# Masked weights transposed in quarters, the last pair amid the first unit of products

## Chip, cores, metric

One core of one Trainium2 chip. The time is that of the device in microseconds (us); of several runs the median is given.

## The reference

`x` is (128, 32, 128): 128 batches of 32 tokens with 128 features; `cond_8` is (128, 8). Two layers, each added to its input, in 32-bit floats:

```python
# layer 0: a weight matrix for each batch, mixed from 8 masked ones
masked_w = weight * mask[None, :, :]                  # (8, 128, 128)
w_bot = jnp.einsum('bg,got->bot', y, masked_w)        # y = cond_8
x = x + (jnp.einsum('bnt,bot->bno', x, w_bot) + bias)
# layer 1: 8 experts, the top 2 of softmax(cond_8) for each batch, and a shared MLP
rw = softmax(cond_8); w, sel = top_k(rw, 2); w = w / w.sum(-1)
out = sum over e of dense_w[:, e] * gemma_mlp(x, skill_gate[e], skill_up[e], skill_down[e])
x = x + out + gemma_mlp(x, shared_gate, shared_up, shared_down)
```

`gemma_mlp` is `(gelu(x @ gate) * (x @ up)) @ down` with 512 hidden features.

## The kernel before, in words

All data lie transposed, with features on the 128 partitions and the 4096 tokens along the free side. The work has a short opening (layer 0 for all batches, with the routing of the experts done beside it on VectorE) and a long rest (the shared MLP over eight tiles of 512 tokens, and tiles of gathered tokens for the experts), which is TensorE work almost without a pause. The order of instructions on each engine is the order of the program text: the schedule is written out by hand, and generators (`make_weights`, `routing`) let parts of one step be put between parts of another.

The change touches the opening only. Its steps:

- **Loads** (L89 to L96). SP issues the conditions, the mask and three eighths of the weights `w0_sb`; ScalarE's queue issues the other five eighths.
- **Warm-up** (`warm_up`, L105). Products of ones with ones into a bank that nobody reads, six at L109 and three at L217. Each appears as two records on TensorE.
- **`spread_cond`** (L220). VectorE spreads the transposed conditions in `ps_y` into `yd`, which is what the products of the units stream: the first 32 batches at L230, the other 96 at the end of `transpose_weights` (L262).
- **Masks** (L238 to L245). VectorE multiplies the weights by the mask into `mw`, in two halves of 512 elements per partition.
- **Transposes** (`transpose_weights`, L248). Eight transposes of 128x128 on TensorE, in pairs; each pair goes to one PSUM bank, and the bank is copied to `wT` (L261), pair 0 and 2 by ScalarE, 1 and 3 by VectorE. The four banks come from the pools `ps_g` and `ps_u` in turn.
- **Units** (`make_weights`, L271). A unit makes half of the weights of 32 batches. It takes four banks, and for each of four values of `k` issues four matrix products, one for each group of 32 rows (`j`), each into another bank; a 32-bit product is two records, so that a unit has 32. Products of different row groups run beside each other. Then the four banks are evicted to `W` with a reordering copy: `j` = 0 and 2 by ScalarE (L294), `j` = 1 and 3 by VectorE (L292). Unit 1 reads the first half of `wT` (pairs 0 and 1), unit 2 the second (pairs 2 and 3), and so on in turn for the next 32 batches.
- **Banks.** PSUM has eight: two in the pool `ps_g`, three in `ps_u`, three in `ps_o`. In a pool the buffers are handed out in turn. `bank` (L266) takes the next pool from `ring` (L264), the names "guouoguo" repeated. A tile can be written once the buffer's former tile has been read for the last time. `warm` took a buffer of `ps_u` and `ps_y` one of `ps_o`.
- **`apply_weights`** (L297). For a tile of 512 tokens, 16 batches, products of `W` with the tokens (L303), copied by ScalarE to `z`; `finish_cond` (L316) transposes `z` back and adds bias and tokens. Three units come first, then the tiles 0 and 1 (which need units 1 and 2), some routing steps (`advance`), then the second `hold_loads` (L182, a memset by VectorE which SP waits for), the loads of the shared weights, two more units, and so on (L760 to L778).

Of the kernel before, what the change touches and what calls it, by code (L numbers as in the profile page):

```python
# [10 lines left out]
F32 = mybir.dt.float32  # L11
# [19 lines left out]
def kernel(  # L31
# [16 lines left out]
    nc = tc.nc  # L48
    P = 128
    D, NT = xT.shape  # L50
    B, G = cond.shape
# [21 lines left out]
    const = ctx.enter_context(tc.tile_pool(name="const", bufs=1))  # L73
# [8 lines left out]
    ps_g = ctx.enter_context(tc.tile_pool(name="ps_g", bufs=2, space=PSUM))  # L82
    ps_u = ctx.enter_context(tc.tile_pool(name="ps_u", bufs=3, space=PSUM))
# [16 lines left out]
    ident = const.tile([P, P], F32, name="ident")  # L100
# [4 lines left out]
    def warm_up(n):  # L105
        for _ in range(n):
            nc.tensor.matmul(warm[:, 0:P], ones, ones, start=True, stop=True)
# [50 lines left out]
    OQ = RG // G  # L158
    NJ = P // RG
    OB = OQ * NJ  # L160
    NQ = P // OB
# [52 lines left out]
    nc.tensor.transpose(  # L214
        ps_y[:, 0:B], cond_rep.rearrange("b j g o -> b (j g o)"), ident
    )
    warm_up(3)  # L217
    yd = const.tile([P, B, OQ], F32, name="yd")

    def spread_cond(b0, n):  # L220
        nc.vector.tensor_tensor(
            yd[:, b0 : b0 + n, :],
            ps_y[:, b0 : b0 + n].unsqueeze(2).to_broadcast([P, n, OQ]),
            own4.unsqueeze(1).to_broadcast([P, n, OQ]),
            ALU.mult,
        )

    QB = TB // P
    NB = TB // (QB * OQ)
    spread_cond(0, NB)  # L230


    NR = P // OQ
    mw = const.tile([P, NR, G, OQ], F32, name="mw")
    w0_r = w0_sb.rearrange("p g (r o) -> p r g o", o=OQ)
    mask_r = mask_sb.rearrange("p (r o) -> p r o", o=OQ)
    NRH = NR // 2
    for half in range(2):  # L238
        rows = ts(half, NRH)
        nc.vector.tensor_tensor(  # L240
            mw[:, rows, :, :],
            w0_r[:, rows, :, :],
            mask_r[:, rows, :].unsqueeze(2).to_broadcast([P, NRH, G, OQ]),
            ALU.mult,
        )  # L245
    wT = const.tile([P, NQ, P], F32, name="wT")

    def transpose_weights():  # L248
        TQ = QB // 2
        for i in range(NQ // TQ):  # L250
            pool, tag = (ps_u, "u") if i % 2 else (ps_g, "g")
            pt = pool.tile([P, TQ * P], F32, name="pt", tag=tag)
            for k in range(TQ):
                q = i * TQ + k
                nc.tensor.transpose(  # L255
                    pt[:, ts(k, P)],
                    mw[:, ts(q, NJ), :, :].rearrange("p j g o -> p (j g o)"),
                    ident,
                )
            copy = nc.vector.tensor_copy if i % 2 else nc.scalar.copy  # L260
            copy(wT[:, ts(i, TQ), :].rearrange("p q t -> p (q t)"), pt)  # L261
        spread_cond(NB, B - NB)  # L262

    ring = itertools.cycle("guouoguo")  # L264

    def bank(name):  # L266

        pool, tag = {"g": (ps_g, "g"), "u": (ps_u, "u"), "o": (ps_o, "acc")}[next(ring)]
        return pool.tile([P, TB], F32, name=name, tag=tag)

    def make_weights(i, half):  # L271

        banks = [bank(f"w_{j}") for j in range(NJ)]
        q0 = half * QB
        for k in range(QB):
            for j in range(NJ):
                rows = slice(j * RG, (j + 1) * RG)
                nc.tensor.matmul(  # L278
                    banks[j][:, ts(k, NB * OQ)],
                    wT[rows, q0 + k, :],  # L280
                    yd[rows, ts(i, NB), :].rearrange("p b o -> p (b o)"),
                    start=True,
                    stop=True,
                )
        yield
        for j in range(NJ):
            dst = W[:, ts(i, NB), q0 * OB : (q0 + QB) * OB].rearrange(
                "p b (k o) -> p k b o", k=QB
            )[:, :, :, ts(j, OQ)]
            src = banks[j].rearrange("p (k b o) -> p k b o", k=QB, o=OQ)  # L290
            if j % 2:
                nc.vector.tensor_copy(dst, src)  # L292
            else:
                nc.scalar.copy(dst, src)  # L294
        yield
# [312 lines left out]
    class Pipeline:  # L608
# [31 lines left out]
        def copy(self):  # L640
            other = Pipeline(self.h_pool)
            other.pending = list(self.pending)
            return other
# [15 lines left out]
    def shared_tile(t, widths=None):  # L659
        def finish(ps, part):  # L660
            w = part.stop - part.start
            cols = slice(t * TB + part.start, t * TB + part.stop)
            if t < EARLY:
                nc.vector.tensor_tensor(acc[:, cols], ps[:, 0:w], x1[:, cols], ALU.add)
            elif t < NTILE - 2:
                nc.vector.tensor_tensor(acc[:, cols], ps[:, 0:w], acc[:, cols], ALU.add)
            else:
                o = o_pool.tile([P, w], F32, name="o", tag="o")
                nc.vector.tensor_tensor(o, ps[:, 0:w], acc[:, cols], ALU.add)  # L669
                queue = nc.scalar if part.start else nc.sync  # L670
                queue.dma_start(out=outT[:, cols], in_=o)

        return Mlp(TB, x1[:, ts(t, TB)], shared, finish, widths)
# [76 lines left out]
        return mlp  # L750


    units = [make_weights(i, half) for i in range(B // NB) for half in range(2)]

    def weights():
        unit = units.pop(0)
        next(unit)
        next(unit)

    transpose_weights()  # L760
    PAIR = NB // BT
    for _ in range(3):
        weights()
    for i in range(2):
        for t in range(PAIR):
# [50 lines left out]
    between = shared_tile(EARLY)  # L816
# [90 lines left out]
```

## Time and profile before

| | |
|---|---|
| median of three runs | 285.27 us (285.13 to 285.67) |
| profiled execution | 284.8 us |
| its span, first to last instruction | 283.1 us |
| mean granted TensorE clock | 1.000 |
| TensorE busy | 277.5 us |
| first mask multiplication (L240) starts | 4.82 us |
| first product of a unit (L278) starts | 6.75 us |
| first eviction on VectorE (L292) starts | 7.99 us |
| first product of `apply_weights` (L303) starts | 10.57 us |

In the rows of the profile PE is TensorE's products, PEld its weight loads, DVE VectorE, ACT ScalarE, POOL GpSimd, SP the engine that issues most of the DMAs. A row of the timeline gives start and duration in us, engine, line, operation, the tiles written and read, their shape, the number of instructions merged in the row, and in brackets how long the engine was idle before and what it waited for. Instructions on TensorE overlap: a row's duration is from the start of its first to the end of its last, gaps between starts can hide in it. The chain of waits is followed back from the last instruction, at each step to what released it.

### The profile page before, as it was taken

To read this page: it belongs to the slowest core of one execution; us is meant where nothing else is said; L and a number is where in the kernel's file an instruction comes from. 1 tells how busy PE (TensorE), PEld (TensorE's weight loads), DVE (VectorE), ACT (ScalarE), POOL (GpSimd) and SP (SyncE) were. 2 spreads that over 40 slices of the span, in tenths; PEclk is the share of its full clock that TensorE was granted. 3 is DMA by queue.
4 is the path that set the end of the run, shared out by engine and by line. 5 is a ranking of instruction groups with operands and counts; after the bars stand their busy time and mean duration, and the time that the engine had idled before them with its cause. 6 is when DMAs were issued, how large, how long until landed. Compare 5 with 4: busy or idle time off the path is not lost.

```text
span 283.1 us, 5164 instructions
## 1 busy us (share of the span) xinstructions
PE 277.5 (98%) x1424; PEld 171.8 (61%) x1424; DVE 166.9 (59%) x489; ACT 78.8 (28%) x149; POOL 47.9 (17%) x285
## 2 busy tenths in 40 slices
PE   7999999999999999999999999999999999999994
PEld 6987545657657567576585665765557444444442
DVE  4897794546666666666566676666666733233232
ACT  5665123222222222222222222222222221222120
POOL 3001213423024220241222212421000000000000
PEclk9999999999999999999999999999999999999999
DMA  4381067334335435325253343432000020100101
GB/s 129 108 220 45 2 190 255 115 111 121 105 112 166 132 111 151 113 94 168 85 182 106 112 151 111 127 115 96 5 0 1 14 97 0 39 0 3 71 37 45
DMA packets 25763, 27.21 MB, mean 96 GB/s; under 512 B 1920, under 2 KB 16768, under 8 KB 25728
## 3 DMA queue, kind: packets, MB, share of 16 engines
q1 hardware_dynamic: 25440, 26.42, 29.9%
q10 hardware_dynamic: 288, 0.39, 0.5%
q8 instruction: 13, 0.21, 0.3%
q14 instruction: 22, 0.18, 0.2%
HBM read 24.71 MB, written 2.10 MB: 95 GB/s over the span
## 4 chain that ended last, share of the span: by engine, by line
PE 96%; DMA 1%; DVE 0%; SPq 0%; issue 0%; DVEq 0%
PE pg L580 30%; PE pu L580 30%; PE ps_out L598 29%; PE w L278 3%; PE pz L303 3%; PE pt L320 1%; DMA w_sb<-in_w0T_dram 1%; PE pt L255 0%; DVE mw L240 0%; PE ps_w L544 0%; SPq L92 0%; SPq L90 0%; DVE o L669 0%; PE ps_i L543 0%; PE ps_n L370 0%
## 5 line engine op out<-in xcount | busy, mean ns | idle before, releaser
L587 DVE TENSOR_TENSOR h<-ge,pu 128x384 f32<-128x384 f32 (+1 forms) x117 | 69.3, 592 | 76.4 <-PE pu L580 76.4
L585 ACT ACTIVATE ge<-pg 128x384 f32<-128x384 f32 (+1 forms) x117 | 61.4, 525 | 186.1 <-PE pg L580 175.7
L731 DVE SCALAR_TENSOR_TENSOR acc<-ps_out,slot_w,acc 128x32 f32 x260 | 65.1, 250 | 27.6 <-DVE h L587 17.1
L598 PE MATMUL ps_out<-h,wd 128*128 128x384 f32 (+2 forms) x216 | 70.3, 424 | 0.0
L580 PE MATMUL pu<-xg,wu 128*128 128x384 f32 (+2 forms) x216 | 70.0, 423 | 0.0
L580 PE MATMUL pg<-xg,wg 128*128 128x384 f32 (+2 forms) x216 | 70.0, 423 | 0.0
L710 POOL COPY xg<-x 128x32 f32 x260 | 41.9, 209 | 120.3 <-PE pu L580 96.3
L580 PEld LDWEIGHTS pg<-xg,wg 128*128 128x128 f32 x216 | 37.7, 190 | 19.8 <-issue 0.7
L598 PEld LDWEIGHTS ps_out<-h,wd 128*128 128x128 f32 x216 | 37.5, 190 | 20.1 <-DVE h L587 1.3
L580 PEld LDWEIGHTS pu<-xg,wu 128*128 128x128 f32 x216 | 37.6, 190 | 19.1
L580 PE MATMUL pg<-x,swg 128*128 128x512 f32 x64 | 32.8, 594 | 0.0
L580 PE MATMUL pu<-x,swu 128*128 128x512 f32 x64 | 32.7, 592 | 0.0
L598 PE MATMUL ps_out<-h,swd 128*128 128x512 f32 (+2 forms) x72 | 32.4, 545 | 0.0
L598 PEld LDWEIGHTS ps_out<-h,swd 128*128 128x128 f32 x72 | 13.3, 190 | 14.9 <-issue 12.4
L580 PEld LDWEIGHTS pu<-x,swu 128*128 128x128 f32 x64 | 12.2, 190 | 15.3 <-issue 15.1
L580 PEld LDWEIGHTS pg<-x,swg 128*128 128x128 f32 x64 | 11.8, 190 | 12.6 <-issue 11.7
L292 DVE COPY W<-w 128x512 f32<-128x512 f32 x16 | 9.9, 682 | 0.7 <-PE w L278 0.7
L294 ACT COPY W<-w 128x512 f32<-128x512 f32 x16 | 8.3, 598 | 3.7 <-PE w L278 3.7
L278 PE MATMUL w<-yd,wT 32*128 32x128 f32 x256 | 9.0, 279 | 0.0
L278 PEld LDWEIGHTS w<-yd,wT 32*128 32x128 f32 x256 | 8.2, 186 | 1.2 <-DVE x L321 0.8
L325 POOL COPY acc<-x 128x512 f32<-128x512 f32 x6 | 3.7, 614 | 29.7 <-DVE x L321 29.5
L303 PE MATMUL pz<-W,xin 128*32 128x128 f32 x256 | 7.8, 274 | 0.1
(99 smaller groups left out, 67.7 us busy)
## 6 DMA issues: line engine op xcount, KB each, us to landing
wg<-in_gate_dram SPq DMA_DIRECT2D x27, 256.0 KB, 2.8
wu<-in_up_dram SPq DMA_DIRECT2D x27, 256.0 KB, 2.9
wd<-in_down_dram SPq DMA_DIRECT2D x27, 256.0 KB, 2.8
xin<-in_xT_dram SPq DMA_DIRECT2D x6, 256.0 KB, 4.3
out_dram<-acc SPq DMA_DIRECT2D x4, 256.0 KB, 2.1
xin<-in_xT_dram SPq DMA_DIRECT2D x1, 512.0 KB, 6.5
out_dram<-acc SPq DMA_DIRECT2D x1, 512.0 KB, 2.6
w_sb<-in_w0T_dram ACTq DMA_DIRECT2D x1, 320.0 KB, 2.9
```

The source lines that it names most:

```text
L278: nc.tensor.matmul(banks[j][:, ts(k, NB * OQ)], wT[rows, q0 + k, :], yd[rows, ts(i, NB), :].rearrange("p b o -> p (b o)"), start=True, sto ...
L292: nc.vector.tensor_copy(dst, src)
L294: nc.scalar.copy(dst, src)
L303: nc.tensor.matmul(pz[j * N : (j + 1) * N, ts(k, P)], x_sb[t][:, ts(b, N)], W[:, t * BT + b, :], start=True, stop=True,)
L320: nc.tensor.transpose(pt[:, ts(k, P)], z[:, ts(k, P)], ident)
L325: nc.gpsimd.tensor_copy(acc[:, ts(t, TB)], x1[:, ts(t, TB)])
L580: nc.tensor.matmul(ps[:, ts(i, self.n)], w[:, ts(c, P)], self.x_in, start=True, stop=True,)
L585: nc.scalar.activation(ge[:, 0:n], pg[:, 0:n], AF.Gelu_apprx_tanh)
L587: nc.vector.tensor_tensor(h[:, 0:n], ge[:, 0:n], pu[:, 0:n], ALU.mult)
L598: nc.tensor.matmul(ps[:, 0 : cols.stop - cols.start], self.wd[:, c, :], h[:, i * self.n + cols.start : i * self.n + cols.stop], start=(c = ...
L710: nc.gpsimd.tensor_copy(xg[:, ts(j, N)], x1[:, bass.ds(v, N)])
L731: nc.vector.scalar_tensor_tensor(a, ps[:, ts(j, N)], slot_w[:, slot0 + j : slot0 + j + 1], a, ALU.mult, ALU.add,)
```

## The change

The masks are multiplied in four quarters instead of two halves. After each of the first three quarters its pair of transposes is issued. The fourth quarter's pair is issued in the middle of unit 1, between its second and third value of `k`. All four pairs are copied to `wT` by ScalarE: three ahead of unit 1, the fourth between the products and the evictions of unit 1. The second `spread_cond` follows the fourth mask. The four banks of the pairs are taken up front. The ring starts with "ouogguou" for units 1 and 2 and then goes on as before. The second warm-up has one product instead of three.

```diff
-    warm_up(3)
+    warm_up(1)
...
-    NRH = NR // 2
-    for half in range(2):
-        rows = ts(half, NRH)
+    wT = const.tile([P, NQ, P], F32, name="wT")
+    TQ = 2
+    TR = TQ * NJ
+    pts = [
+        pool.tile([P, TQ * P], F32, name="pt", tag=tag)
+        for pool, tag in ((ps_g, "g"), (ps_u, "u")) * (NQ // TQ // 2)
+    ]
+
+    def mask_weights(i):
+        rows = ts(i, TR)
         nc.vector.tensor_tensor(
             mw[:, rows, :, :],
             w0_r[:, rows, :, :],
-            mask_r[:, rows, :].unsqueeze(2).to_broadcast([P, NRH, G, OQ]),
+            mask_r[:, rows, :].unsqueeze(2).to_broadcast([P, TR, G, OQ]),
             ALU.mult,
         )
-    wT = const.tile([P, NQ, P], F32, name="wT")
-
-    def transpose_weights():
-        TQ = QB // 2
-        for i in range(NQ // TQ):
-            pool, tag = (ps_u, "u") if i % 2 else (ps_g, "g")
-            pt = pool.tile([P, TQ * P], F32, name="pt", tag=tag)
-            for k in range(TQ):
-                q = i * TQ + k
-                nc.tensor.transpose(
-                    pt[:, ts(k, P)],
-                    mw[:, ts(q, NJ), :, :].rearrange("p j g o -> p (j g o)"),
-                    ident,
-                )
-            copy = nc.vector.tensor_copy if i % 2 else nc.scalar.copy
-            copy(wT[:, ts(i, TQ), :].rearrange("p q t -> p (q t)"), pt)
-        spread_cond(NB, B - NB)
-
-    ring = itertools.cycle("guouoguo")
+
+    def transpose_weights(i):
+        for k in range(TQ):
+            nc.tensor.transpose(
+                pts[i][:, ts(k, P)],
+                mw[:, ts(i * TQ + k, NJ), :, :].rearrange("p j g o -> p (j g o)"),
+                ident,
+            )
+
+    def copy_transpose(i, copy):
+        copy(wT[:, ts(i, TQ), :].rearrange("p q t -> p (q t)"), pts[i])
+
+
+    ring = itertools.chain("ouogguou", itertools.cycle("guouoguo"))
...
-    def make_weights(i, half):
+    def make_weights(i, half, between=None):
...
         for k in range(QB):
+            if between and k == QB // 2:
+                between()
             for j in range(NJ):
...
-    units = [make_weights(i, half) for i in range(B // NB) for half in range(2)]
+    units = [
+        make_weights(i, half, None if (i, half) != (0, 0) else lambda: transpose_weights(3))
+        for i in range(B // NB)
+        for half in range(2)
+    ]
...
-    transpose_weights()
+    for i in range(3):
+        mask_weights(i)
+        transpose_weights(i)
+    mask_weights(3)
+    spread_cond(NB, B - NB)
+    for i in range(3):
+        copy_transpose(i, nc.scalar.copy)
+
+    unit = units.pop(0)
+    next(unit)
+    copy_transpose(3, nc.scalar.copy)
+    next(unit)
     PAIR = NB // BT
-    for _ in range(3):
+    for _ in range(2):
         weights()
```

## The prediction

> **What bounds the kernel now.** I read the page's busy table and its chain first, then the chain of waits up to 20 us in order of time, then the timeline of the first 12 us, the last one opened in windows of a few tenths of a us so that single instructions have their own start.
>
> ```profile
> PE 277.5 (98%) x1424; PEld 171.8 (61%) x1424; DVE 166.9 (59%) x489; ACT 78.8 (28%) x149; POOL 47.9 (17%) x285
> ...
> PE 96%; DMA 1%; DVE 0%; SPq 0%; issue 0%; DVEq 0%
> ```
>
> TensorE is busy 98% of the span and carries 96% of the chain. Nothing behind 10.57 us interrupts the chain for long, so whatever the change does to the time at which the products of `apply_weights` (L303) begin reaches the end of the kernel nearly undiminished. The opening decides. Its chain:
>
> ```profile
> 1.74 2.96 DMA w_sb<-in_w0T_dram
> ...
> 4.82 0.70 DVE mw L240
> ...
> 5.57 1.26 PE pt L255 x8
> 6.82 3.66 PE w L278 x94
> ...
> 10.57 1.95 PE pz L303 x64
> ```
>
> The weights land at 4.70, VectorE masks, TensorE transposes, the units of L278 follow. The row of 3.66 us hides what matters: a unit is 32 products, and the first takes from 6.753 to 7.748, so three would take 2.98 us plus tails. The timeline shows who is really late:
>
> ```profile
> 4.82 1.29 DVE L240 TENSOR_TENSOR mw<-w_sb,mask_sb 128x512 f32<-128x512 f32 x2 [0.21 <-DMA w_sb<-in_w0T_dram]
> ...
> 6.75 3.73 PE L278 MATMUL w<-yd,wT 32*128 32x128 f32 x96
> ...
> 7.94 2.05 ACT L294 COPY W<-w 128x512 f32<-128x512 f32 x4 [0.93 <-PE w L278]
> 7.99 3.68 DVE L292 COPY W<-w 128x512 f32<-128x512 f32 x6 [0.24 <-PE w L278]
> ...
> 10.57 1.95 PE L303 MATMUL pz<-W,xin 128*32 128x128 f32 x64
> ```
>
> VectorE's six evictions stand without a gap: start 7.986, ends 8.677, 9.273, 9.872, 10.468. The first waits for the end of the first unit. Call its start D = 7.986. `apply_weights(0)` needs the fourth eviction: 10.468, and its first weight load stands at 10.539, its first product at D + 2.58. Unit 3 needs banks that unit 1 held: its weight loads wait until 8.58 (ScalarE's eviction ended 8.530), 8.729 (VectorE's first, 8.677), 9.067 (ScalarE's second, 9.016) and 9.325 (VectorE's second, 9.273). From 9.325 it needs 0.885 us to its last product at 10.210. So TensorE could go on at about 10.41; the fourth eviction is later by 0.15. Two paths, 0.15 apart, both hung on D.
>
> **Masks in quarters.** Two multiplications of 512 elements (0.687 us, starts 0.609 apart) become four of 256. No row shows that one. The nearest is VectorE's copy of 128x256 at 0.424 us, with the next instruction 0.342 behind its start; half of 0.687 is the lower bound, 0.344. I take 0.42 and a spacing of 0.342: starts 4.82, 5.16, 5.50, 5.85, ends 5.24, 5.58, 5.93, 6.27. TensorE starts 0.052 behind a mask (5.511 to 5.563), and the second transpose of a group 0.165 behind its first: pairs at 5.29/5.46, 5.64/5.80, 5.98/6.14. The first half was done at 5.511 before.
>
> **Copies by ScalarE.** Four copies of 128x256 at 0.372 us replace two there and two on VectorE. ScalarE is free from 5.677. The first starts 0.037 behind its transpose's end (5.46 + 0.273), so 5.77 to 6.14, the next 6.14 to 6.51, then to 6.89. The first unit's first half needs the first, its second half the second; both are in time. The fourth waits for the late transposes (7.17 + 0.273, below): 7.48 to 7.85. Behind it in ScalarE's queue stands only the first eviction, which can't start before 8.1, and unit 2's fourth load, which takes its bank, is due at 7.91: nothing. On VectorE two copies (0.85 us) go and `spread_cond` (0.545) moves up to 6.19 to 6.73. That is worth nothing now: VectorE idled 0.24 before its first eviction anyway. It removes a small wait of unit 2, whose fourth load stood until 7.800 for `spread_cond`'s end at 7.748; unit 2 isn't late for anybody.
>
> **The transposes amid the first unit.** A change between 128-row and 32-row products costs TensorE time in every case of the trace: 6.550 to 6.753, 12.251 to 12.454, 14.250 to 14.451, 15.270 to 15.473, 19.291 to 19.492, always 0.20 where neighbours of one kind stand 0.11 apart; and the second round behind a change comes 0.21 later instead of 0.11. So: 6.14 + 0.203 = 6.345 for the unit's first round (0.41 earlier than 6.753), rounds at 6.56, 6.67, 6.78 (to 6.80 for the last row group); change 0.20, transposes at 7.00 and 7.17; change 0.20, rounds at 7.37, 7.58, 7.69, 7.80. The last product of VectorE's bank is at 7.81 against 7.643. **The head start of 0.41 us is more than eaten: D becomes 8.15, later by 0.17.** The Trainium skill says otherwise in "TensorE: Matmul & The Clock Gate", step-by-step part of "What happens when you issue a matmul": the reorder window pulls weight loads ahead of running products if row groups don't conflict or the spare weight buffer is used, so a change would be free. By that rule all would follow 0.11 apart: rounds at 6.25 to 6.58, transposes at 6.69 and 6.80, rounds at 6.91 to 7.24, and D would be 7.59, earlier by 0.39. A 128-row load conflicts with all row groups, and the five places show 0.20: I follow the rows.
>
> **The ring of banks.** The new first eight names are o u o g, g u o u. In each pool the buffers go round, which the four waits of unit 3 above confirm one by one. Counting: the `ps_u` buffers are taken by `warm`, transposes 1 and 3, unit 1 (0), unit 2 (1 and 2), and unit 3 gets 0 and then 1. So unit 3's fourth bank is the one that unit 2's second product group held, and that is VectorE's *third* eviction; before it was the second. Its first bank (`ps_g` 0) also waits for VectorE, the second eviction (before: ScalarE's first), so unit 3 stands at its first load and all later TensorE work is queued behind it in order. The fourth load comes at D + 1.886 + 0.052 = D + 1.94, the last product 0.885 later, the change to L303 0.203: products of L303 at D + 3.03. The path through the fourth eviction stays D + 2.58. The order of the two paths turns round, and the change costs 3.03 - 2.58 = 0.45 us whatever D is.
>
> Behind it VectorE's last two evictions end 1.38 us after L303 begins, 1.10 before; the routing steps and the memset at 13.18 that releases SP's shared loads follow 0.28 later relative to TensorE. VectorE had 0.45 us idle before 13.687, and the loads at L202 to L204 (to landing 2.7 to 4.1 us from 13.88) are wanted at 20.42: nothing more on the path. POOL gets nothing new, SP issues the same DMAs.
>
> **Fewer warm-up products.** Four records go (4.487 to 5.096). The clock column reads 1.00 in all stretches, but starts of the warm-up products stand 0.214 apart at 4.07 and 0.111 apart from 4.487: TensorE is at half speed until about 4.47. The two kept end as the fast clock begins; those removed run in idle time ahead of 5.29. By the row the cost is nothing. The same page, "The HAM clock gate", speaks against it: the warm-up is about 3.4 us of activity in a window that runs freely, not a number of products; in an execution whose window ends later, idle time of 0.64 us (4.65 to 5.29, before 0.47 to 5.56) could leave it half full. If the clock rose one such window later, at 7.9, spacings up to there double and the unit ends about 0.83 later: 1.44 us in all. I take nothing and keep 1.44 as the upper end.
>
> **Sum.** D + 0.17, and 0.45 for the bank: L303 begins at 11.18 instead of 10.57, +0.61 us. The profiled execution took 284.8 us for a span of 283.1, so it would take 285.4. It lies 0.47 below the median of the runs, 285.27, to which I add the difference: 285.9 us. About 0.2% (0.57 us) is what a measurement of this kernel can tell from no change; the forecast lies just above.
>
> **Rivals.** (1) *The changes between row sizes are free, as the rule says.* D = 7.59, but the bank still decides: L303 at 10.62, 0.05 late, 285.3: same. Against it the five places. (2) *The bank doesn't bind, so the forecast ends on the other side, not slower.* Then the fourth eviction decides as before: 285.27 + 0.17 = 285.4 with paid changes, 285.27 - 0.39 = 284.9 with free ones. The point from which it decides: both paths are equal when unit 3's fourth load comes at D + 2.58 - 0.203 - 0.885 = D + 1.49, so when the eviction that frees its bank ends by D + 1.44; the second does (D + 1.29), the third (D + 1.89) doesn't. For it: a mistake by one buffer in my count suffices. (3) *The clock rises later*: 285.27 + 1.44 = 286.7. For it the lost activity; against it that the step at 4.47 comes ahead of what is removed. (4) *The change doesn't do what it says*: the quarters come no sooner, since the four masks share one engine and the last still ends at 6.27 (before 6.11); the gain of 0.41 exists only through the split of the unit. A gain over 0.57 us I can't build: even with changes of row size free and no bank in the way D falls 0.39.
>
> **Chances.** The forecast 0.58 (0.36 above the bound, 0.22 below it, as 0.61 lies at the bound and the runs spread over 0.54 us), rival 1 0.10 (same), rival 2 0.14 (0.12 same, 0.02 faster), rival 3 0.12 (slower), something faster that the trace doesn't show 0.06. Slower 0.48, same 0.44, faster 0.08. The range leaves out rival 2's free end and most of the clock case, and takes in the rest: 285.1 to 286.5; the likeliest case's own is 285.6 to 286.2.
>
> **What would show it.** Right: L278's first product near 6.35, two transposes amid unit 1 with 0.20 on both sides, the first eviction near 8.15, the fourth load of unit 3 released by VectorE's third eviction near 10.1, L303 near 11.2. Wrong: an eviction before 7.99 (changes are cheap), L303 within 0.1 of the fourth eviction's end (the bank doesn't bind), or transposes 0.21 apart behind 5.3 (the clock). What would make it wrong most cheaply is the bank count.

## The result, and the profile after

The changed kernel takes 286.06 us (median of 22 runs, 285.45 to 287.83) against 285.23 us before (22 runs): the ratio is 1.004, 95% interval 1.0027 to 1.0053. Slower, as forecast, and 0.16 us from the forecast 285.9. But the 22 times are not one heap. Twelve lie at 285.45 to 286.15 (median 285.73), ten at 287.27 to 287.83 (median 287.55), none between; the median stands at the upper edge of the lower group. That it does so is luck: with one of the twelve in the upper group it would be 286.6, outside the range of 285.1 to 286.5. The forecast describes the lower group: 0.50 us above before, 0.61 predicted. The upper group is the rival that was given 12%.

The profiled execution of after (285.85 us, span 284.1) belongs to the lower group. Its busy row and its chain, from the page:

```profile
PE 277.9 (98%) x1420; PEld 171.3 (60%) x1420; DVE 166.3 (59%) x489; ACT 79.4 (28%) x151; POOL 47.9 (17%) x285
...
PE 97%; DVE 1%; issue 0%; DVEq 0%
```

TensorE still carries all but the opening. The chain of waits of its opening (start, duration):

```profile
5.29 1.26 PE pt L255 x6
6.55 0.66 PE w L281 x16
7.21 0.37 PE pt L255 x2
7.58 0.74 PE w L281 x16
8.31 1.88 DVE W L295 x3
...
10.23 1.15 PE w L281 x26
11.39 1.89 PE pz L306 x64
```

Before, the chain ran from L278 to L303 on TensorE alone. Now three evictions of VectorE stand in it, and TensorE takes over at 10.23, when the third of them has ended (8.31 + 1.88 = 10.19). The timeline of the same stretch shows both sides:

```profile
4.81 1.43 DVE L246 TENSOR_TENSOR mw<-w_sb,mask_sb 128x256 f32<-128x256 f32 x4
...
6.48 0.73 PE L281 MATMUL w<-yd,wT 32*128 32x128 f32 x16
7.14 0.44 PE L255 MATMUL pt<-ident,mw 128*128 128x128 f32 x2
7.51 1.69 PE L281 MATMUL w<-yd,wT 32*128 32x128 f32 x48
...
8.29 2.48 DVE L295 COPY W<-w 128x512 f32<-128x512 f32 x4 [1.58 <-PE w L281]
9.64 0.31 PEld L281 LDWEIGHTS w<-yd,wT 32*128 32x128 f32 x6 [0.64 <-DVE W L295]
10.23 0.96 PEld L281 LDWEIGHTS w<-yd,wT 32*128 32x128 f32 x26 [0.29 <-DVE W L295]
...
11.26 1.29 DVE L295 COPY W<-w 128x512 f32<-128x512 f32 x2 [0.48 <-PE w L281]
11.32 1.96 PE L306 MATMUL pz<-W,xin 128*32 128x128 f32 x64
```

The first unit begins 0.27 us earlier than before (6.48 for 6.75), and VectorE's first eviction 0.31 later (8.29 for 7.99), idle for 1.58 us ahead of it. VectorE's six copies, gapless before, now fall apart into four and two. TensorE's weight loads of unit 3 wait twice for VectorE, 0.64 and 0.29 us. From L306 on the shift is handed through: the first product of the shared MLP stands at 21.17 instead of 20.42, 0.75 later, just as L306 (11.32 for 10.57).

### The profile page after: what moved, and what is told of

It is laid out like the page before. It is cut to its first block, busy times and chain, and to the rows that moved or that the text cites. A ratio compares the mean times of both kernels' runs of the same rounds, so it can differ in the third digit from the quotient of the medians.

```text
span 284.1 us, 5157 instructions
## 1 busy us (share of the span) xinstructions
PE 277.9 (98%) x1420; PEld 171.3 (60%) x1420; DVE 166.3 (59%) x489; ACT 79.4 (28%) x151; POOL 47.9 (17%) x285
## 4 chain that ended last, share of the span: by engine, by line
PE 97%; DVE 1%; issue 0%; DVEq 0%
PE pg L583 29%; PE pu L583 29%; PE ps_out L601 29%; PE w L281 3%; PE pz L306 3%; PE pt L323 1%; PE warm L107 1%; DVE W L295 1%; PE pt L255 1%; PE ps_w L547 0%; DVE mw L246 0%; PE ps_y L214 0%; DVE o L672 0%; DVE yd L221 0%; DVE ones L99 0%
## 5 line engine op out<-in xcount | busy, mean ns | idle before, releaser
L306 PE MATMUL pz<-W,xin 128*32 128x128 f32 x256 | 7.8, 274 | 0.0
```

Source lines behind the costliest of these rows:

```text
L306: nc.tensor.matmul(pz[j * N : (j + 1) * N, ts(k, P)], x_sb[t][:, ts(b, N)], W[:, t * BT + b, :], start=True, stop=True,)
```

## The experiments

Each kernel is the changed one or the one before with the edit shown. Ratios are to the kernel before on the same chip, with 95% intervals; they are not the quotients of the medians given.

**e1, three warm-up products.**

```diff
-    warm_up(1)
+    warm_up(3)
```

> The changed kernel with its three warm-up products back; nothing else differs. Theory 1 (two costs: the bank and the changes of row size cost about 0.6 us in every execution; the missing warm-up leaves the clock at half speed for one more 3.4 us stretch in about half of them, which costs about 1.7 us more): the group of executions above 287 us disappears, all lie at 285.5 to 286.3, median about 285.85, ratio to before 1.002. The clock rises ahead of about 6 us. Rival (the slow group comes from the new order of banks, copies and transposes): about half of the executions stay above 287 us.

286.13 us (7 runs, 285.65 to 286.36), ratio 1.0026 (1.0015 to 1.0037). No execution lies in the upper group, as theory 1 has it, though seven are few (e12 is the same kernel once more); the size (0.84 over the 285.29 of before on this chip) is 0.2 above what was expected. The clock in the profiled execution rose as expected: TensorE's products stand 0.21 apart up to 5.5 and 0.11 apart soon behind.

**e2, the kernel before with fewer warm-up products.**

```diff
-    warm_up(3)
+    warm_up(1)
```

> The kernel before with one warm-up product instead of three at L217; nothing else differs. Theory 1: masks in halves leave TensorE idle from about 4.9 to 5.56 us, longer than in the changed kernel, so about half of the executions or more lie 1.7 us above before (about 286.9), the others at 285.2. Rival (order, not warm-up): no execution differs from before, 285.2.

286.54 us (22 runs), ratio 1.0027 (1.0013 to 1.0041), in two groups: nine at 284.84 to 285.43 (median 285.35), thirteen at 286.36 to 287.48 (median 286.74). The edit alone makes an upper group, and in the other executions it costs nothing that shows. The group stands 1.4 above the lower one, 1.7 was expected. No execution of it was profiled: the profile of e2, and that of e8, are of the lower group.

**e3, another order of banks** (on top of e1). Unit 2's names become u g o u.

```diff
-    ring = itertools.chain("ouogguou", itertools.cycle("guouoguo"))
+    ring = itertools.chain("ouogugou", itertools.cycle("guouoguo"))
```

> The changed kernel with three warm-up products and the second four of the ring as u g o u instead of g u o u, so that unit 3's fourth bank is one that ScalarE evicts first of unit 2 instead of VectorE's third eviction. Theory 1: unit 3's fourth load comes at D + 1.57 instead of D + 1.94 (D is the start of VectorE's first eviction, about 8.15), L303 begins at about D + 2.66 = 10.8, the time is 0.37 us below the same kernel with the old ring: 285.5. Rival (the bank doesn't bind, L303 is held by the fourth eviction or by TensorE's own work): no difference to e1, 285.85.

285.74 us (22 runs), ratio 1.0014 (1.0007 to 1.0021), 0.39 below e1: as expected. In its profile products stand 0.11 apart from about 4.4 on, so that the split shows there without a change of the clock:

```profile
6.37 0.73 PE L281 MATMUL w<-yd,wT 32*128 32x128 f32 x16
7.03 0.44 PE L255 MATMUL pt<-ident,mw 128*128 128x128 f32 x2
...
7.40 1.69 PE L281 MATMUL w<-yd,wT 32*128 32x128 f32 x48
...
8.18 3.89 DVE L295 COPY W<-w 128x512 f32<-128x512 f32 x6 [1.43 <-PE w L281]
...
10.84 1.95 PE L306 MATMUL pz<-W,xin 128*32 128x128 f32 x64
```

With D = 8.182 the fourth load of unit 3 stands at 9.754, D + 1.57, and L306 at D + 2.66, both the expected numbers; VectorE's six copies are one row again, 3.89 us long against 3.68 before. In after, L306 began at D + 3.02. The bank costs what it was said to. Over all traces L306 stands 3.02 or 3.03 us behind D where the ring is as changed and the clock is up by then (after, e1, e4, e6, e12), and 2.65 to 2.67 with u g o u (e3, e5, e9, e10, e11).

**e4, no split** (on top of e1, ring as changed).

```diff
-        make_weights(i, half, None if (i, half) != (0, 0) else lambda: transpose_weights(3))
+        make_weights(i, half)
...
     mask_weights(3)
+    transpose_weights(3)
     spread_cond(NB, B - NB)
```

> The changed kernel with three warm-up products and the fourth pair of transposes ahead of unit 1 instead of amid it; ring as changed. Theory 1 (each change of row size costs TensorE): first product of a unit at 6.69 instead of 6.35, yet D at 7.93 instead of 8.15, L303 at D + 3.03 = 10.96, 285.6: 0.2 us below e1. Rival (changes are cheap when loads are pulled ahead, the split hides the wait for the fourth mask): D at least 0.1 later than in e1, 286.0 or more.

285.59 us (21 runs), ratio 1.0008 (1.0001 to 1.0014), 0.54 below e1: theory 1 in sign and above it in size. The profiled execution can't be used for D: in it products stood 0.21 apart up to 7.08.

**e5, all three undone** (e4 with the ring of e3).

> Quarters and ScalarE's copies kept, all three costly parts undone: three warm-up products, the fourth pair of transposes ahead of unit 1, and the ring with u g o u for unit 2. Theory 1 (warm-up, bank and changes of row size are the whole loss): D at 7.93 with the clock up in time, L303 at the later of D + 2.58 and D + 2.66 = 10.59, time as before, 285.2 to 285.4. Rival (quarters or ScalarE's four copies cost something of their own): 285.6 or more.

285.44 us (22 runs) against 285.5, ratio 0.999 (0.998 to 1.0). Nothing of the loss is left: the quarters and ScalarE's four copies cost nothing, and gain nothing that these runs can tell.

**e6, no second warm-up product** (the changed kernel with `warm_up(0)`).

> The changed kernel with no second warm-up product at all. Theory 1 (idle TensorE ahead of the first transposes makes the clock wait for another 3.4 us stretch): more than the half of the executions that the changed kernel has lie above 287 us, a profiled one of these has its products 0.21 apart until after 8 us. Rival (number of products doesn't matter): half, as in the changed kernel.

287.09 us (20 runs), ratio 1.0033 (1.0018 to 1.0048): nine at 285.46 to 285.91, eleven at 287.07 to 287.50. This is a miss for the count: about half, as with one product, not more, though 11 of 20 and 10 of 22 are too few to tell two shares apart. The rest held: the profiled execution is of the upper group (287.17), and its transposes and both halves of unit 1 stand at twice the spacing, with VectorE's first eviction at 9.86.

**e7 and e8, other executions of the same kernels.**

> The changed kernel itself once more, to profile another execution. Theory 1: with an even chance it is one of the slow group, about 287.5 us; then its transposes and the rounds of units 1 and 2 stand at twice the spacing until one 3.4 us stretch later than the clock otherwise rises. If the slow group had another cause, a slow execution would show the fast spacing from 6 us on.

> The kernel before with one warm-up product, once more, to profile another execution. Theory 1: with a chance of 13 in 22 it is one of the slow group at about 286.7 us, with products at twice the spacing until 8 us or later. Rival: a slow one shows the fast spacing from 6 us on.

e8 gave 285.0 us, an execution of the lower group, with its transposes and products 0.11 apart from their start at 5.6 on. e7 gave 287.84, an execution of after's upper group. Its timeline:

```profile
5.24 1.54 PE L255 MATMUL pt<-ident,mw 128*128 128x128 f32 x6 [0.43 <-DVE mw L246]
...
6.71 1.24 PE L281 MATMUL w<-yd,wT 32*128 32x128 f32 x16
...
7.88 0.69 PE L255 MATMUL pt<-ident,mw 128*128 128x128 f32 x2
...
8.50 3.14 PE L281 MATMUL w<-yd,wT 32*128 32x128 f32 x54
...
9.80 2.71 DVE L295 COPY W<-w 128x512 f32<-128x512 f32 x4 [3.14 <-PE w L281]
...
13.05 1.95 PE L306 MATMUL pz<-W,xin 128*32 128x128 f32 x64
```

The same 16 records take 1.24 us instead of 0.73, the pair of transposes 0.69 instead of 0.44. Opened by single instructions, the transposes stand 0.213 apart, unit 1's rounds 0.214, and unit 2's too, into its last rounds at 10.6. VectorE begins at 9.80 instead of 8.29, and L306 at 13.05 instead of 11.32: 1.73 us, against 1.82 between the groups' medians. The chain of this execution starts like that of after; its work is the same, only TensorE's pace differs.

**e9 to e12, the split doubled, and the others beside it on one chip.** e9 is e3 with one transpose of the fourth pair ahead of unit 1's third value of k and the other ahead of its fourth; e10 is e3, e11 is e5, e12 is e1.

```diff
-            if between and k == QB // 2:
-                between()
+            if between and k >= QB // 2:
+                between(k - QB // 2)
...
-    def transpose_weights(i):
-        for k in range(TQ):
+    def transpose_weights(i, ks=range(TQ)):
+        for k in ks:
...
-        make_weights(i, half, None if (i, half) != (0, 0) else lambda: transpose_weights(3))
+        make_weights(i, half, None if (i, half) != (0, 0) else lambda k: transpose_weights(3, [k]))
```

> Three warm-up products, the ring with u g o u for unit 2, and the split doubled: one of the fourth pair's transposes ahead of unit 1's third value of k, the other ahead of its fourth, so four changes of row size instead of two. Theory 1 (each pair of changes costs TensorE about 0.2 us at full clock, more where the clock is still half): D 0.24 later than in e10, the time 0.24 to 0.45 us above e10, 0.4 to 0.9 above e11. Rival (the split costs by its place, not by the changes of row size, for instance through the late fourth copy): no difference to e10.

> The same kernel as e3 (three warm-up products, u g o u, one split), beside the others on one chip. Theory 1: 0.2 to 0.45 us above e11 (no split), 0.37 us below e12 (old ring).

> The same kernel as e5 (three warm-up products, u g o u, no split). Theory 1: within 0.2 us of the kernel before, the lowest of the four; with the clock up by 5.3 us its D is 7.93.

> The same kernel as e1 (three warm-up products, ring as changed, one split), for more executions. Theory 1: 0.6 us above before, 0.37 above e10, none above 287 us, so that the rest of the changed kernel's loss is the warm-up's.

| | split | unit 2's banks | us (runs) | ratio to before |
|---|---|---|---|---|
| e9 | two | u g o u | 286.11 (6) | 1.0037 (1.0024 to 1.0051) |
| e12 | one | g u o u | 286.20 (11) | 1.0026 (1.0014 to 1.0038) |
| e10 | one | u g o u | 285.72 (21) | 1.0014 (1.0003 to 1.0025) |
| e11 | none | u g o u | 285.17 (14) | 0.9997 (0.9987 to 1.0008) |

The order is theory 1's, and no execution of e12 lies above 286.64. e10 to e11 is 0.55, e9 to e10 0.39, e12 to e10 0.48, with overlapping intervals. Why e1 and e12 lie 0.8 us above before, where after's lower group lies 0.5 above, is not shown; their executions with a late rise of the clock, which in after may be those of the upper group, would go that way. The traces tell the split more sharply, if D is counted from the start of the first mask (the landing of the weights differs between executions). e9 first:

```profile
5.13 1.43 DVE L246 TENSOR_TENSOR mw<-w_sb,mask_sb 128x256 f32<-128x256 f32 x4 [0.52 <-DMA w_sb<-in_w0T_dram]
...
7.30 0.33 PE L255 MATMUL pt<-ident,mw 128*128 128x128 f32 x1
...
7.56 0.50 PE L281 MATMUL w<-yd,wT 32*128 32x128 f32 x8
...
7.99 0.33 PE L255 MATMUL pt<-ident,mw 128*128 128x128 f32 x1
...
8.25 1.69 PE L281 MATMUL w<-yd,wT 32*128 32x128 f32 x40
...
8.81 3.90 DVE L295 COPY W<-w 128x512 f32<-128x512 f32 x6 [1.79 <-PE w L281]
```

and e11, without a split:

```profile
5.21 1.43 DVE L246 TENSOR_TENSOR mw<-w_sb,mask_sb 128x256 f32<-128x256 f32 x4 [0.52 <-DMA w_sb<-in_w0T_dram]
...
5.69 1.44 PE L255 MATMUL pt<-ident,mw 128*128 128x128 f32 x8
...
7.06 2.07 PE L281 MATMUL w<-yd,wT 32*128 32x128 f32 x64
...
8.30 3.89 DVE L295 COPY W<-w 128x512 f32<-128x512 f32 x6 [1.19 <-PE w L281]
```

From the first mask to D: 3.09 us without a split (e11), 3.33 with one (e3; 3.35 in e10, the same kernel), 3.69 with two (e9). So the first split costs 0.24 and the second 0.36. This holds only where the clock is up early enough: e5, the same kernel as e11, took 3.37, as its clock rose 1.68 us behind the first mask, against 1.21 in e11, where the last pair of transposes waited for its mask anyway. The unit in one piece ends earlier than in two, although it starts later.

## Why the prediction was right, and where it failed

**Masks.** Four quarters at 0.417 to 0.426 us, about 0.34 apart, ending at 5.24, 5.57, 5.91 and 6.24: within 0.03 of the sum.

**The split.** Rounds, transposes and rounds stood in e3 at 6.37, 7.03 and 7.40 (6.35, 7.00, 7.37 predicted), D at 8.18 (8.15), with 0.20 at each change. The reorder window that the prediction cites from the Trainium skill ("TensorE: Matmul & The Clock Gate", "What happens when you issue a matmul") did not make these changes free; the page names two conditions for pulling a load ahead, and that a change then costs nothing was the prediction's own inference. In the timed runs the split costs 0.5 (e10 to e11) where the clean traces have 0.24; the intervals admit both. That a change costs more while the clock is still half, 0.37 in e7 from the last round to the first transpose, would go that way, but this was not tried by itself.

**The bank.** The fourth load of unit 3 stood at D + 1.94 and L306 at D + 3.02 in after: the predicted terms to 0.01. e3 removed the wait, and with it 0.39 us. Rival 2 falls.

**The profiled sum.** L306 lies 0.75 late, not 0.61. The missing 0.14 is in D, 8.295 for 8.15: in this execution the transposes stood 0.21 apart until 6.0, so that they and ScalarE's first copies were late, and the first unit began at 6.48 for 6.345.

**The warm-up is the step that failed:** "By the row the cost is nothing ... I take nothing". The row was of one execution, in which the clock rose at 4.47, ahead of the products that were to go. That time moves from one execution to the next. Each trace file holds it, though no view prints it: with three products 4.43 (e3) to 7.15 (e4), with one 4.33 (e2), 4.89 (e8), 6.13 (after) or 10.71 (e7), with none 10.23 (e6). The clock column could not have shown it, as it reads 1.00 ahead of the rise too, and so does the mean of 1.000 of the kernel before. For the same stretch of after and of e7 (its ends, its length, TensorE's busy time and records, then the clock):

```profile
6.10:8.50 2.40, 2.40 (x54) 1.00 0.89 262
...
6.10:8.50 2.40, 2.40 (x22) 1.00 0.91 278
```

The removed products decide in nearly every second execution: 10 of 22 in after, 13 of 22 in e2, 11 of 20 in e6. Of the executions with three products only 3 of 124 (e1, e3 to e5, e9 to e12) lie more than 1 us above the median of their kernel, and 8 of 166 of the kernel before. The window of activity that runs freely (the Trainium skill, "TensorE: Matmul & The Clock Gate", "The HAM clock gate"), about 3.4 us long, spoke for this and was put at 12%.

**Why every second one.** In all fourteen traces the full clock lasts 80, 81 or 82 times 3.4133 us (e7 273.07, after 276.48, before 279.89): it rises and falls on a grid of 3.41 us, as the page has it, and the grid lies elsewhere in each execution. Counted back from the rise, this gives the earlier edges. How full the stretches between them were can be estimated if each record of TensorE ahead of the rise counts for 0.213 us, the spacing at which records follow each other there, and overlaps count once:

| | products | stretches without a rise: filled | stretch before the rise: filled |
|---|---|---|---|
| after | one | to 2.72: 0.42 | 2.72 to 6.13: 0.75 |
| e4 | three | 0.32 to 3.73: 0.71 | 3.73 to 7.15: 0.93 |
| e6 | none | to 3.40: 0.62; 3.40 to 6.82: 0.58 | 6.82 to 10.23: 0.82 |
| e7 | one | 0.47 to 3.88: 0.75; 3.88 to 7.30: 0.69 | 7.30 to 10.71: 0.86 |

In all fourteen every stretch before a rise was filled to 0.75 or more by this count, and every one without a rise to 0.75 or less. e4 and e7 have almost the same edges: with three products the stretch was full enough, with one it was not, and the clock waited for the next edge. Where an edge falls early, the stretch holds most of the first warm-up (0.86 in e2, 0.87 in e8), and nothing is lost. So it is the place of the grid that picks the executions, and the missing products that leave the stretch too empty. This was read from the traces afterwards and no run was made to test it; whether the share grows without any product stays open.

**Its size** was off as well. The sum let the spacing double up to 7.9, one stretch behind 4.47, and gave 0.83 us more than without it. But the executions that lose are those whose edge falls later: in e7 the edge at 7.30 was missed, the spacing was double through all of units 1 and 2, to 10.7, and L306 came 1.73 later than in after. Rival 3's 286.7 should have been about 287.6.

None of the kernels beats the one before beyond its interval; e5 and e11 come out even.

## What to carry to other kernels

Before a step is moved into the middle of another on TensorE, count the changes between row sizes that it adds: the two here took back the head start of 0.33 us (first product of a unit 1.52 us behind the first mask in e3, 1.85 in e11) and 0.24 us more. When names of banks are reordered, follow each buffer one round further than the edit, to the unit that takes it next, and see which eviction of which engine frees it. Judge warm-up products by many executions, not by one trace: look for two groups in the times, and for the clock in the spacing of the products.

## What was not expected of the hardware

The time at which TensorE's spacing halves moved by some 6 us between executions of nearly the same opening (4.43 in e3, 10.71 in e7), on a grid of 3.41 us, and this made a difference of 1.8 us at the end (1.82 between after's groups). Transposes seem to count as activity for it: without them e4's stretch before its rise would be filled to 0.47 only, where 0.75 was too little in e7 (0.47 to 3.88, which holds no transposes of the weights). The landing of the first weights varied too: the first mask began between 4.76 and 5.21 us.
